# Layer 1's first tile without row gathers behind its exponentials, and the experts' first up weights behind the last 1/sum

## The chip, the cores and the metric

The kernel runs on one core of a Trainium2 chip. The metric is the device time of one execution in microseconds (us). A core has five engines with queues of their own: PE (TensorE, matrix products; its weight loads are listed as PEld), DVE (VectorE), ACT (ScalarE), POOL (GpSimd) and SP (SyncE, which here only issues transfers). Each works through its queue in order; they wait for each other through semaphores.

## The reference, cut to what matters

Four layers. Each adds a cross attention to `x` (4 batches of 512 tokens, 128 wide) and then a mixture of experts; each block reads a layer norm of `x`. The context has 4 batches of 154 rows. The four attentions and expert blocks differ in detail. Layers 1 to 3 look like this:

```python
x = x + xattn(layernorm(x), ctx)     # 16 heads; layer 1: 8 wide, layers 2 and 3: 64 wide
#   energy = q k^T * scale ; attn = softmax(energy) ; out = (attn @ v) @ Wo
x = x + ffn(layernorm(x))            # 8 experts
#   logits = x @ Wg ; the best expert (layer 1) or the best two (layers 0, 2, 3) of each token
#   y = act(x @ W1[e] + b1) @ W2[e] ; out = sum of weight * y
```

Layer 0's experts are gated (two up weights of 128 by 512 and SiLU), those of layers 1 and 3 are 128 by 512 (GELU, ReLU), those of layer 2 128 by 256 (GELU). Everything is float32.

## The kernel before

**Tokens and tiles.** `x` stays in SBUF as four tiles `x[b]` of 128 partitions by 4 by 128. An attention goes through 16 tiles of 128 queries, `(b, i)` with `b` the batch and `i` the quarter of it; they are counted 0 to 15 here.

**The attention of layers 1 to 3.** The class `Tile` holds the steps of one tile. `score(g)` (g = 0, 1, 2) makes the scores of up to six heads on PE; `most(g)` takes minus their row maxima on DVE (L309); `exp(g)` exponentiates them on ACT, head by head, and sums the rows (L323). `inverse` takes 1/sum on DVE (L347). `replicate` brings 1/sum into the shape of the transposed output: a transpose on PE (L352), a copy `rT` on DVE (L354), a transfer `rd` to DRAM and one or two transfers `rep` back that repeat each row for the channels of its head (L359 and L360 in layer 1, L363 and L365 in layers 2 and 3). `turn(n)` transposes four heads' weights on PE (L388), `take(n)` copies them to SBUF as `pT` (L279 on DVE, L282 on ACT), `by_v(n)` multiplies them by the values (L425). `turn_ends`, `take_ends` (`tails`) and `by_v_ends` do that for the last 26 of the 154 context rows. `scaled` multiplies by `rep` (L432, `aT`), `project` is the output projection (L442), `residual` adds to `x`.

**The period.** Two tiles are worked on at a time. `narrow_period` (layer 1) and `wide_period` (layers 2 and 3) write out one period: the scores and exponentials of the new tile between the transposes and products of the old one. In layer 1 a tile's `replicate` comes in the period of the next tile and its projection in the one after that; in layers 2 and 3 `replicate` comes at the end of the tile's own period. `attend_all` loops over the 16 periods. The period calls hooks: `parts` prepares the next batch (norm, keys, values), `middle` and `after` call `step`, which goes one step further in a generator `beside`. In the first periods `beside` is the combination of the layer before, from the tile `(2, 0)` on it is the routing of the first half of the tokens. When `b == 1 and i == 0`, `beside` is finished and the statistics of batches 2 and 3 are taken; the norm of batch 2 stands in `parts` of tile (1, 1).

**The experts.** The tokens are handled in two halves (batches 0 and 1, batches 2 and 3). `route` computes norm, logits, the best experts and each token's slot, and puts one scatter for each tile and choice on the list `rows_due` (L752, an indirect DMA on POOL). `experts` goes through blocks of 128 slots: `load` fetches four blocks of tokens when all scatters are done (L870), `tokens` transposes them on PE (L882), `up` reads the block's expert number into registers of SP and PE, loads this expert's up weights (L901, `w`, three buffers) and multiplies (L909), `down` applies the activation, multiplies by the down weights (L948), copies (L957) and stores to `ybuf` (L960). In layers 1 to 3 two blocks go together (`PER`), a pair; one buffer `w` holds one pair's weights. `load_down` fetches all down weights of a layer in one transfer of 2 MB (1 MB in layer 2; L852).

**Row transfers.** `gather` puts the way back on `rows_due` too: for each tile and choice one indirect DMA on POOL (L993) that fetches the rows from `ybuf`, after all stores. `combine` adds them to `x` with their weights (L1017). `row_transfers(n, behind)` starts the next `n` of the list and makes each of them wait for the instruction `behind`, so that they are spread: two behind each `pT` copy, `2 * n` behind each copy of `down`. In layer 1, three more stand behind each of the three `exp(g)` of tile 0, so that of the 16 gathers of layer 0's second half nine go behind tile 0's exponentials and seven behind the `pT` copies in the period of tile 1.

**Who sets the order.** The program is built with `schedule_with_timeline_sim=True`: a planner orders each engine's queue by its own estimate of times, in favour of what comes first in the program. Within `tc.manual_schedule(engines=...)` the queues named keep the program's order: PE and ACT in the attention of layer 1 (`ordered`), PE, ACT and DVE in that of layers 2 and 3 (`ordered_all`). All else is the planner's: DVE in layer 1's attention, SP and POOL everywhere, and all queues in the experts' stages.

**From the attention to the experts.** After `attend_all` the program starts `experts(layer, 0, ...)` by one step (tokens and the first pair's weights and products), then writes the last tile's remaining period (`narrow_period(None, last, older=late)` or `wide_period(None, last)`; `last` is tile 15 and `late` tile 14), then alternates two steps of the second half's routing with one of the first half's experts.

Of the kernel before, what the change touches and what calls it, by code (L numbers as in the profile page):

```python
# [30 lines left out]
GROUPS = (((0, 1), (2, 3)),) * 4  # L31
# [6 lines left out]
PER = (1, 2, 2, 2)  # L38
# [18 lines left out]
def tile_xattn_moe_stack(ctx: ExitStack, tc: tile.TileContext, a: dict, out: bass.AP):  # L57
# [10 lines left out]
    nc = tc.nc  # L68
# [216 lines left out]
    class Tile:  # L285
# [31 lines left out]
        def exp(self, g):  # L317
            if g == 0:
                self.pr = p2.tile([P, H, S2], F32, tag="probs", name="probs")
            for s in range(min(3, 8 - 3 * g)):  # L320
                for j in range(2):
                    h = self.at.heads(None, 3 * g + s, j)
                    ins = nc.scalar.activation(  # L323
                        self.pr[:, h, :],
                        self.sc[g][:, j, s * S2 : (s + 1) * S2],
                        AF.Exp,
                        bias=self.nm[:, h : h + 1],
                        accum_out=self.rs[:, h : h + 1],
                    )
            if self.at.dh < 64 and self.at.first and self.i == 0:  # L330
                row_transfers(3, ins)

        def short(self):
            if self.nb == 1:
# [14 lines left out]
        def replicate(self):  # L349

            q = ps_tr()
            nc.tensor.transpose(q[0:H, 0:P], self.rinv, ident)  # L352
            rT = small.tile([H, P], F32, tag="rT", name="rT", bufs=2)
            nc.vector.tensor_copy(rT, q[0:H, 0:P])  # L354
            self.rep = p2.tile([P, self.nb, P], F32, tag="rep", name="rep", bufs=1)
            dh = self.at.dh
            if self.nb == 1:
                rd = dram.tile([P, P], F32, tag="rd8", name="rd8", bufs=4)
                nc.sync.dma_start(rd.rearrange("(h d) q -> h d q", d=dh), bc(rT, 1, dh))  # L359
                nc.sync.dma_start(self.rep[:, 0, :], rd)  # L360
            else:
                rd = dram.tile([H, P], F32, tag="rd", name="rd", bufs=4)
                nc.sync.dma_start(rd, rT)  # L363
                for j in range(self.per):
                    nc.sync.dma_start(  # L365
                        self.rep[j * dh : (j + 1) * dh],
                        rd.rearrange("(c j) q -> j c q", j=self.per)[j].partition_broadcast(dh),
                    )


        def turn_ends(self):
# [288 lines left out]
    def row_transfers(n=2 * MOST, behind=None):  # L660

        for start in rows_due[:n]:
            ins = start()
            if behind is not None:
                wait_for(ins, (behind,), "spread over the work beside it")
        del rows_due[:n]
# [185 lines left out]
        nc.sync.dma_start(t[:, :, 0:nf, :], a[f"down{layer}"].rearrange("p (e c d) -> p e c d", e=E, c=nf))  # L852
        return t

    def experts(layer, half, routed, w2):

        ebs, _, scatters = routed
        nj, nf, nu = most_blocks(layer, half), NF[layer], UPS[layer]
        per = PER[layer]
        pack = a[f"up{layer}"]  # L860
# [26 lines left out]
        def up(blocks):  # L887

            w = wff.tile([P, 1032], F32, tag="w", name="w")
            w = w[:, 0 : per * width].rearrange("p (b n) -> p b n", b=per)  # L890
            sc = ps_sc()
            es = []
            for b, j in enumerate(blocks):
                e = nc.values_load(
                    ebs[0:1, j : j + 1],
                    engines=[mybir.EngineType.SP, mybir.EngineType.PE],
                    min_val=0,
                    max_val=E - 1,
                    skip_runtime_bounds_check_because="a count of at most E - 1, by a minimum",
                )  # L900
                nc.sync.dma_start(w[:, b, :], pack[bass.ds(e, 1), :, :].rearrange("o p n -> p (o n)"))  # L901
                es.append(e)
            for b, j in enumerate(blocks):
                xT = toks[j // 4][:, (j % 4) * P : (j % 4 + 1) * P]
                for u in reversed(range(nu)):
                    for fc in range(nf):
                        at = (u * nf + fc) * P
                        dst = sc[:, u if per == 1 else b, fc * P : (fc + 1) * P]
                        nc.tensor.matmul(dst, w[:, b, at : at + P], xT, start=True, stop=True)  # L909
            return es, w, sc  # L910
# [230 lines left out]
    def layer1_setup():  # L1141
# [24 lines left out]

        def prepare(b, found):
            at = Attention()
            at.dh, at.wo, at.first = dh, woT, b == 0

            def masks_in():
                if b == 0:
# [195 lines left out]
    def attend_all(layer, prepare, found, at, beside):  # L1368

        old = older = None
        period = narrow_period if layer == 1 else wide_period
        busy[0] = layer == 1
        with tc.manual_schedule(engines=ordered if layer == 1 else ordered_all):
            new = Tile(at, 0)
            if layer == 1:  # L1380
                new.score(0)
                new.most(0)
            for b in range(B):
                new_at = prepare(b + 1, found) if b < B - 1 else None
                for i in range(NI):
                    at_n, i_n = (at, i + 1) if i < NI - 1 else (new_at, 0)
                    nxt = Tile(at_n, i_n) if at_n else None
                    step = nothing if (b, i) in ((0, 0), (2, 0)) or layer > 1 and (b, i) == (0, 1) else beside.step

                    def queries(i=i, at=at):  # L1390
                        if i < NI - 1:
                            at.queries(i + 1)

                    def parts(i=i, new_at=new_at):
                        if new_at:
                            for part in new_at.parts[i]:
                                part()
                            if i == NI - 1:
                                new_at.queries(0)

                    def after(b=b, i=i, step=step):
                        step()
                        if GROUPS[layer - 1][1][0] == 1 and b == 0 and i == 1:
                            found[1] = stats(x[1])
                        if b == 1 and i == 0:
                            beside.finish()
                            found.update({k: stats(x[k], layer == 2) for k in range(2, B)})

                    period(new, old, nxt, step, queries, parts, after, older)
                    if b == 2 and i == 0:  # L1410
                        beside = Steps(route(layer, 0, *gates[layer]))
                    older, old, new = old, new, nxt
                at = new_at
        busy[0] = False
        return beside.finish(), old, older
# [15 lines left out]
    for layer in range(4):  # L1431
        w2 = load_down(layer)
        if layer == 0:
            result, second = attend_first(layer, prepare, found)
            last = None
        else:
            result, last, late = attend_all(layer, prepare, found, at, beside)
            second = Steps(route(layer, 1, *gates[layer]))
        routed = [result]
        row_transfers()  # L1440
        if 0 < layer < 3:
            prepare = setups[layer + 1]()
        first = Steps(experts(layer, 0, routed[0], w2)).step(2 // PER[layer])
        if layer == 1:
            narrow_period(None, last, older=late)
            last.project()
            last.residual()
        elif last:
            wide_period(None, last)
        while not second.done:  # L1450
            second.step(2)
            first.step(2 // PER[layer])
        routed.append(second.result)
        stores = first.finish()
        row_transfers()
        got = gather(layer, 0, routed[0], stores)
        if layer < 3:
            if layer == 0:
                prepare = setups[1]()
            at = prepare(0, found)  # L1460
            for part in at.early:
                part()
        second = Steps(experts(layer, 1, routed[1], w2)).step((9, 3, 5, 5)[layer])
        for k, b in enumerate(GROUPS[layer][0]):
            for i in range(NI):
                combine(layer, 0, k, i, routed[0], got)
            if layer < 3:
                found[b] = stats(x[b], layer == 1)
            else:
                nc.sync.dma_start(out_v[b], x[b])  # L1470
            second.step(2 // PER[layer])
        if layer < 3:
            for part in at.late:
                part()
            at.queries(0)
        stores = second.finish()
        beside = Steps(combining(layer, routed[1], gather(layer, 1, routed[1], stores)))
# [33 lines left out]
```

## Time and profile before

| what | value |
|---|---|
| median of 6 runs | 1266.0 us (1263.77 to 1272.77) |
| the profiled execution | 1272.21 us, its span 1270.5 us |
| mean granted TensorE clock | 0.932 |
| busy share of the span | PE 85%, PEld 70%, DVE 57%, ACT 44%, POOL 20% |
| chain that ended last | PE 59%, DVE 14%, DMA 9%, issue 7%, POOL 5%, ACT 5% |
| layer 1's attention, first and last scores (L1236) | 253.7 to 465.5 us |
| the 16 gathers in it (L993) | first issued at 264.7, last at 284.6 us |
| first expert products (L909) of layers 1, 2, 3 | 470.58, 798.55, 1133.35 us |

A row of a timeline gives start, duration, engine, line, operation and output<-inputs, how many instructions were merged, and in brackets how long the engine had been idle before it and what ended that. A row of the chain of waits gives start, duration and who. Instructions of DMA on SP and POOL are the issues; the landing comes later. Times are from the span's start.

### The profile page before, as it was taken

Reading aid. Unit: us, or ns where it says so; the run is one execution under the profiler, and the core shown is the slowest. Engines: PE = TensorE matmul, PEld = TensorE weight load, DVE = VectorE, ACT = ScalarE, POOL = GpSimd, SP = SyncE. Lnnn points to the kernel's source line nnn. Section 1 sums busy time; section 2 is a strip of 40 time slices with the busy share of each in tenths; the row PEclk is TensorE's granted clock in tenths of the full one; section 3 lists DMA queues with packets and bytes.
Section 4 is the critical chain, followed back from the end, with each engine's and each line's share of the span. In section 5 each row is a group of like instructions: output and inputs, shape, how many; then the busy total and the mean of one; then the engine's idle time right before and its main releaser. Section 6 shows DMA issues by size and latency. Waiting matters only on the chain.

```text
span 1270.5 us, 26420 instructions
## 1 busy us (share of the span) xinstructions
PE 1085.5 (85%) x9412; PEld 890.8 (70%) x9412; DVE 730.1 (57%) x2012; ACT 564.2 (44%) x2264; POOL 252.6 (20%) x281
## 2 busy tenths in 40 slices
PE   6877998958878788879999998976899999899990
PEld 4657997924444457778878777865778787789880
DVE  6655547567776753235666776524476576646352
ACT  2204333454554554346556565321656665532220
POOL 2041405050000200212000013045220000402334
PEclk9788999988998988989999999887899999999996
DMA  7025776630011313532112214444421111444762
GB/s 230 1 78 151 223 237 187 207 114 12 13 25 34 86 50 110 158 110 52 35 36 67 51 39 122 136 148 128 126 56 43 43 35 36 110 108 139 214 182 60
DMA packets 136064, 126.77 MB, mean 100 GB/s; under 512 B 12538, under 2 KB 115583, under 8 KB 135551
## 3 DMA queue, kind: packets, MB, share of 16 engines
q1 hardware_dynamic: 128767, 110.39, 31.0%
q0 software_dynamic: 7168, 14.69, 4.0%
q8 instruction: 77, 1.26, 0.4%
q14 instruction: 52, 0.43, 0.1%
HBM read 101.31 MB, written 23.72 MB: 98 GB/s over the span
## 4 chain that ended last, share of the span: by engine, by line
PE 59%; DVE 14%; DMA 9%; issue 7%; POOL 5%; ACT 5%; SPq 2%; POOLq 0%; DVEq 0%; ACTq 0%
PE sc L909 10%; PE av L948 7%; PE tr L388 6%; PE av L425 6%; PE sc L625 5%; PE tr L442 5%; DMA yg<-ybuf,su 3%; PE sc L610 3%; ACT probs L323 3%; DVE nm L309 3%; POOL yg L993 3%; PE sc L1236 2%; DMA w<-in_up 2%; POOL buf L752 2%; PE av L407 2%
## 5 line engine op out<-in xcount | busy, mean ns | idle before, releaser
L323 ACT ACTIVATE probs<-sc,nm 128x154 f32<-128x154 f32 x768 | 286.3, 402 | 163.3 <-DVE nm L309 161.4
L909 PE MATMUL sc<-tokT,w 128*128 128x128 f32 x1528 | 198.8, 283 | 12.9 <-DMA w<-in_up 6.5
L909 PEld LDWEIGHTS sc<-tokT,w 128*128 128x128 f32 x1528 | 186.9, 198 | 18.7 <-ACT eg L932 5.9
L309 DVE TENSOR_REDUCE nm<-sc 128x6 f32<-128x924 f32 x144 | 142.6, 1007 | 70.6 <-PE sc L625 47.6
L323 ACT ACTIVATION_READ_ACCUMULATOR probs<-sc,nm 128x1 f32 x768 | 168.4, 219 | 0.0
L948 PE MATMUL av<-w,hT 128*128 x1160 | 155.9, 279 | 3.3 <-DVE hT L937 2.7
L993 POOL DMA_INDIRECT yg<-ybuf,su x112 | 107.0, 956 | 244.5 <-issue 68.5
L948 PEld LDWEIGHTS av<-w,hT 128*128 128x128 f32 x1160 | 141.7, 192 | 9.1 <-issue 4.0
L752 POOL DMA_INDIRECT buf<-xn,su x112 | 108.3, 967 | 199.1 <-DVE ve L248 55.3
L250 POOL TENSOR_TENSOR rstd<-ve,nhalf 128x4 f32<-128x4 f32 x32 | 32.9, 1029 | 567.8 <-DVE ve L248 510.0
L279 DVE COPY pT<-tr 128x512 f32<-128x512 f32 x160 | 106.8, 684 | 43.9 <-PE tr L388 40.1
L388 PE MATMUL tr<-ident,probs 128*128 128x128 f32 x768 | 121.8, 289 | 7.8 <-DVE rT L354 7.8
L425 PE MATMUL av<-pT,vm 128*64 128x128 f32 (+1 forms) x1536 | 106.3, 284 | 19.4 <-DVE pT L279 19.3
L388 PEld LDWEIGHTS tr<-ident,probs 128*128 128x128 f32 x768 | 85.1, 145 | 39.4 <-issue 21.3
L425 PEld LDWEIGHTS av<-pT,vm 128*64 128x64 f32 (+1 forms) x1536 | 63.8, 127 | 52.6 <-DVE pT L279 27.4
L932 ACT ACTIVATE eg<-sc,w 128x128 f32<-128x128 f32 x184 | 52.9, 367 | 88.3 <-PE sc L909 83.7
L625 PE MATMUL sc<-kT,qT 64*128 64x154 f32 x1024 | 86.2, 305 | 4.7 <-ACT probs L323 4.7
L625 PEld LDWEIGHTS sc<-kT,qT 64*128 64x128 f32 x1024 | 70.5, 187 | 15.7 <-issue 9.9
L937 DVE SCALAR_TENSOR_TENSOR hT<-sc,w,eg 128x128 f32<-128x128 f32 x184 | 55.9, 341 | 41.1 <-ACT eg L932 41.1
L610 PE MATMUL sc<-xnT,wq 128*128 128x128 f32 x512 | 72.8, 301 | 4.7 <-ACT probs L323 2.3
L610 PEld LDWEIGHTS sc<-xnT,wq 128*128 128x128 f32 x512 | 66.5, 210 | 10.0 <-issue 3.4
L957 DVE COPY ys<-av 128x256 f32<-128x256 f32 (+1 forms) x110 | 38.9, 355 | 54.5 <-PE av L948 50.6
(260 smaller groups left out, 1462.6 us busy)
## 6 DMA issues: line engine op xcount, KB each, us to landing
w<-in_up SPq DMA_DIRECT2D x46, 516.0 KB
w<-in_up SPq DMA_DIRECT2D x76, 258.0 KB
rep<-rd SPq DMA_DIRECT2D x64, 256.0 KB
tok<-buf SPq DMA_DIRECT2D x36, 256.0 KB
ybuf<-ys SPq DMA_DIRECT2D x58, 128.0 KB
w<-in_down SPq DMA_DIRECT2D x3, 2048.0 KB
w<-in_up SPq DMA_DIRECT2D x46, 128.0 KB
ybuf<-ys SPq DMA_DIRECT2D x52, 64.0 KB
```

The lines of the kernel that those rows point to most:

```text
L279: return nc.vector.tensor_copy(o, i)
L309: nc.vector.tensor_reduce(self.at.heads(self.nm, g, n), self.sc[g][:, :, 0 : n * S2].rearrange("p j (s k) -> p j s k", s=n), AX.X, ALU.max ...
L323: ins = nc.scalar.activation(self.pr[:, h, :], self.sc[g][:, j, s * S2 : (s + 1) * S2], AF.Exp, bias=self.nm[:, h : h + 1], accum_out=self ...
L388: nc.tensor.transpose(q[:, t * P : (t + 1) * P], self.pr[:, h, 0:P], ident)
L425: nc.tensor.matmul(av[rows, cols], v, self.pT[n][:, t, :], start=False, stop=last)
L442: nc.tensor.matmul(o[:, 0:D], self.aT[:, c, :], self.at.wo[:, c, :], start=(c == 0), stop=(c == self.nb - 1))
L610: nc.tensor.matmul(sc[:, c // 4, c % 4 * P : (c % 4 + 1) * P], wq[:, c * P : (c + 1) * P], at.xnT[:, i * P : (i + 1) * P], start=True, sto ...
L625: nc.tensor.matmul(sc[:, j, s * S2 : (s + 1) * S2], at.qT[i][rows, c, :], at.kT[rows, c, :], start=True, stop=True)
L752: ins = nc.gpsimd.indirect_dma_start(out=buf[half], out_offset=bass.IndirectOffsetOnAxis(ap=su[:, t : t + 1], axis=0), in_=xns[t // NI][:, ...
L909: nc.tensor.matmul(dst, w[:, b, at : at + P], xT, start=True, stop=True)
L948: nc.tensor.matmul(y[:, b * D : (b + 1) * D], hT[:, fc, :], w2[:, bass.ds(es[b], 1), fc, :].rearrange("p o d -> p (o d)"), start=(fc == 0) ...
L993: ins = nc.gpsimd.indirect_dma_start(out=yg[:, i % NI, :], out_offset=None, in_=ybuf[half][0 : most_blocks(layer, half) * P, :], in_offset ...
```

## The change

Four edits, in the language of the kernel:

1. `Tile.exp` no longer starts row transfers behind the exponentials of layer 1's first tile. The gathers of layer 0's second half now all go two at a time behind `pT` copies: eight in the period of tile 1, eight in that of tile 2.
2. In `attend_all`, `step` does nothing in tile (0, 1) of layer 1 either, as it already did in layers 2 and 3. Layer 0's combination advances in the periods of tiles 2 and 3 instead of 1 and 2.
3. `replicate` keeps its `rep` transfers in `self.sent`. `experts` has a new argument `ahead`; the up loads of the first three pairs of the first half wait for those transfers: tile 14's in layer 1, tile 15's in layers 2 and 3. In layer 0 there are none.
4. A line in `after` goes whose condition (`GROUPS[layer - 1][1][0] == 1`) holds in no layer, since `GROUPS` is ((0, 1), (2, 3)) for all of them.

```diff
@@ Tile.exp
-                    ins = nc.scalar.activation(
+                    nc.scalar.activation(
...
-            if self.at.dh < 64 and self.at.first and self.i == 0:
-                row_transfers(3, ins)
@@ Tile.replicate
-                nc.sync.dma_start(self.rep[:, 0, :], rd)
+                self.sent = [nc.sync.dma_start(self.rep[:, 0, :], rd)]
             else:
...
-                for j in range(self.per):
+                self.sent = [
                     nc.sync.dma_start(
                         self.rep[j * dh : (j + 1) * dh],
                         rd.rearrange("(c j) q -> j c q", j=self.per)[j].partition_broadcast(dh),
                     )
+                    for j in range(self.per)
+                ]
@@ experts
-    def experts(layer, half, routed, w2):
+    def experts(layer, half, routed, w2, ahead=()):
...
-                nc.sync.dma_start(w[:, b, :], pack[bass.ds(e, 1), :, :].rearrange("o p n -> p (o n)"))
+                ins = nc.sync.dma_start(w[:, b, :], pack[bass.ds(e, 1), :, :].rearrange("o p n -> p (o n)"))
+                if j < 3 * per:
+                    wait_for(ins, ahead, "the transfers of the attention's last tile go first")
@@ layer1_setup, prepare
-            at.dh, at.wo, at.first = dh, woT, b == 0
+            at.dh, at.wo = dh, woT
@@ attend_all
-                    step = nothing if (b, i) in ((0, 0), (2, 0)) or layer > 1 and (b, i) == (0, 1) else beside.step
+                    step = nothing if (b, i) in ((0, 0), (0, 1), (2, 0)) else beside.step
...
-                        if GROUPS[layer - 1][1][0] == 1 and b == 0 and i == 1:
-                            found[1] = stats(x[1])
@@ the loop over layers
-        first = Steps(experts(layer, 0, routed[0], w2)).step(2 // PER[layer])
+        ahead = (late if layer == 1 else last).sent if last else ()
+        first = Steps(experts(layer, 0, routed[0], w2, ahead)).step(2 // PER[layer])
```

## The prediction

> **What bounds the kernel now.** Part 4 of the page (the chain that ended last) puts 59% of the span on PE, 14% on DVE and 9% on transfers, but that is an average over four layers; the change touches four places, so I read those. First the table of busy time by stretch, for the start of layer 1's attention; its columns after the width are PE, PEld, DVE, ACT, POOL, the granted clock, DMA share and GB/s.
>
> ```profile
> 262.00:289.00 27.00, 15.76 (x94) 7.25 (x92) 18.55 (x54) 9.86 (x48) 17.07 (x18) 0.76 0.18 50
> 289.00:302.00 13.00, 11.26 (x85) 6.36 (x85) 8.74 (x21) 6.79 (x33) 0.26 (x1) 0.83 0.06 11
> 339.00:351.00 12.00, 9.62 (x85) 4.93 (x85) 8.56 (x17) 6.80 (x33) 0.00 (x0) 1.00 0.06 11
> ```
>
> A later period of this attention takes 11 to 14 us; the one from 262 to 289 takes 27, with no engine full. So something waits there. The chain of waits and the timelines of DVE and PE say what:
>
> ```profile
> 256.27 7.34 DMA ybuf<-ys
> 264.71 0.71 POOL yg L993
> 267.28 0.35 DVE L1017 SCALAR_TENSOR_TENSOR x<-yg,wa,x 128x128 f32<-128x128 f32 x1 [3.83 <-DMA yg<-ybuf,su]
> 270.02 1.11 DVE L309 TENSOR_REDUCE nm<-sc 128x6 f32<-128x924 f32 x1
> 271.05 0.27 DVE L354 COPY rT<-tr 16x128 f32<-16x128 f32 x1
> 271.38 1.11 PE L388 MATMUL tr<-ident,probs 128*128 128x128 f32 x4 [6.96 <-DVE rT L354]
> 284.30 0.65 PE L425 MATMUL av<-pT,vm 128*32 128x128 f32 x8 [3.90 <-DVE pT L279]
> ```
>
> Layer 0's last expert store lands 7.3 us after its issue, behind the 2 MB load of down weights (L852, issued 0.4 us earlier). The row gathers then start one by one, 1.25 us apart. Layer 0's combination (L1017) stands in DVE's queue ahead of the second tile's maxima (L309) and of rT (L354), whose input PE had finished at 263.98. DVE stands still for the rows, and PE stands 6.96 us behind DVE, then 3.90 us more.
>
> Second, the moment where attention hands over to the experts, in layer 2 (queue of SP, PE, POOL):
>
> ```profile
> 771.58 1.19 SPq L901 DMA_DIRECT2D w<-in_up  x2
> 793.03 1.26 SPq L365 DMA_DIRECT2D rep<-rd  x2
> 799.74 6.38 SPq L901 DMA_DIRECT2D w<-in_up  x8
> 798.55 1.16 PE L909 MATMUL sc<-tokT,w 128*128 128x128 f32 x8
> 808.16 1.16 PE L442 MATMUL tr<-wo,aT 128*128 128x128 f32 x8
> 826.43 1.02 POOL L752 DMA_INDIRECT buf<-xn,su  x1 [14.27 <-DVE eb L775]
> 850.75 1.97 PE L882 MATMUL tr<-ident,tok 128*128 128x128 f32 x8 [6.32 <-DMA tok<-buf]
> ```
>
> The first three pairs of up weights (six loads) are in SBUF 20 us before use. PE has expert products (L909) between the last tile's turns, and that tile's last projection (L442) ends only at 809.3. Behind it run the second half's routing, its 16 scatters (20 us on POOL) and its tokens; PE waits 6.32 us for those. Layers 1 and 3 have the same shape, with shorter waits:
>
> ```profile
> 470.58 2.02 PE L909 MATMUL sc<-tokT,w 128*128 128x128 f32 x16 [0.40 <-issue]
> 526.37 0.66 PE L882 MATMUL tr<-ident,tok 128*128 128x128 f32 x4 [2.59 <-DMA tok<-buf]
> 1133.35 2.05 PE L909 MATMUL sc<-tokT,w 128*128 128x128 f32 x16
> 1190.11 0.66 PE L882 MATMUL tr<-ident,tok 128*128 128x128 f32 x4 [1.96 <-DMA tok<-buf]
> ```
>
> **Part 1: gathers and combination.** Nothing is removed but order: 16 gathers, 16 L1017 and the statistics behind them are all still done. Nine gathers lose their place behind tile 0's exponentials (tiles counted from 0, so the table's 27 us are mostly the period of tile 1); in return all 16 go two by two behind the pT copies (L279) of the periods of tiles 1 and 2, and the combination's steps move from tile 1's period to those of tiles 2 and 3.
>
> What goes. (a) The stand before rT: from 263.98 to 271.05, 7.0 us. In the new order rows cannot be asked for before tile 0's first pT copy, so no L1017 can stand before rT or tile 1's second maxima. (b) The rest of tile 1's period: rT to rT is 18.16 us (271.05 to 289.21); the next two are 13.63 and 13.19. I take 13.2 for it: 5.0 us. Together 12.0.
>
> What comes back. 16 L1017 at 0.35 us (5.6) and 8 pairs of L241 and L243 at 0.29 and 0.18 (3.8) are 9.4 us of DVE work. DVE's free time is 4.3 us in the stretch 289 to 302, 4.0 in 302 to 316, and about 13.2 - 8.6 = 4.6 in a normal tile 1: 12.9 in all. It fits, but DVE is in order and each of these can stand before a copy that PE waits for. Bounds: nothing, or all 9.4 us. I take 2.0, about six of the L1017 in the way, nearer to nothing because the room is there. Gain of part 1: 12.0 - 2.0 = 10.0, between 2.6 and 13 (12, and up to 1 where PE ran at half clock: the records grant 0.5 from 269.5 to 276.3 and 283.1 to 293.3).
>
> What hides it: the store's late landing is covered, since it landed at 264.0 and tile 0's first pT copy ends about 266.0 (263.98 plus 0.27, 0.67 and 0.68 for rT, tails and pT, and their handovers). POOL: behind the gathers stand only two rstd (L250), wanted a period later. The gathers will end near 288 instead of 285.5; the combined batches 2 and 3 are first needed by the norm in tile 5's period, after 327. If the rows came later than the order supposes, DVE would stand again: that is the slower rival below.
>
> **Part 2: the held weights.** Six loads each in layers 1, 2 and 3 now wait on SP for a rep transfer to land. Behind a waiting SP stand token groups 2 and 3 (796.38 and 798.06 in layer 2, read at 816.1), later stores, and in layer 1 tile 15's rd and rep (L359, L360; 473.7, 476.1). Those could be up to 2.2 us late (six loads at 0.85 us from 467.7 end at 472.8); rep landed at 478.2 and is read at 486.1, so nothing.
>
> The cost if nothing covers it, from landings in the trace's semaphore records and SP's 0.85 us for each load (four at 425.0 take 2.83 with the last one's 0.33). Layer 1: rep landed 467.7, second load of pair 0 issued 468.6, landed 2.7 later at 471.3, against 470.58: 0.7. Layer 2: rep's second half issued 793.66, landing after 4.3 to 5.4, so near 799; second load at 800, landed 2.1 later at 802.1, against 798.55: 3.5. Layer 3: rep landed 1134.5, second load 1135.4, landed 2.8 later at 1138.2, against 1133.35: 4.9. In all 9.1 us of late experts.
>
> The cover is the attention's last tile, which PE has to do anyway. In layer 2 5.6 us of L909 and L948 lie between 798.55 and L442's end; in layer 3 9.7 us. If these go behind, the last residual and with it the second half's routing, scatters and tokens come earlier, by the 3.5 to 4 us of layer 2 (wait there 6.32), by no more than the 2.5 us of waits for tokens in layer 3 (1.96 and 0.56), and by no more than 2.6 in layer 1: up to 9.1. So part 2 lies between -9.1 and +9.1. I take +1 for layer 1, +2 for layer 2, 0 for layer 3 (PE is 25.92 us busy of the 26 from 1130, so what is moved must be paid there): +3, on the side where a wait is known to be there to be shortened.
>
> [...]
>
> **Sum.** 10 + 3 = 13 us. The profiled execution took 1272.2 (span 1270.5, 1.7 around it), so 1259 for it; it is 6.2 over the median of the six runs, 1266.0, so 1253 for the median. 0.3% is 3.8 us, about what a measurement of this kernel can tell.
>
> **The rivals.** A, the hold is exposed: PE's queue keeps L909 ahead of the last tile's steps, the in-order PE stands for the weights, 9.1 us, and attention stands behind it. Gain 10 - 9.1, time about 1265, between 1260 and 1268. For it: in layer 3 no idle time exists to pay with. Against: the queue order is planned anew, and the planner knows of the wait.
>
> B, slower: the wait for rows is moved, not removed. DVE's queue is in order; if the build places each L1017 right behind the pT copy that releases its rows, DVE stands the gather's 0.3 + 2.5 us (2.4 to 2.5 from issue to landing) at each of 8 pairs: 22 us against 12 saved, 10 slower with part 2 at nothing, 1276. It decides from 5 of the 8 pairs on (14 us). For it: L1017 stands for rows nine times today, 7.8 us. Against: today's order did not know of the late store, which no longer counts.
>
> C, the stand is partly the profiled run's own: that execution is 6.2 over the median. If unprofiled runs have half of the 7.0 and 5.0, the change removes half of what it says: part 1 gives 6 - 2 = 4, with part 2 7, the time is 1259.
>
> **How the numbers follow.** Forecast 0.70 (1246 to 1260 by itself), A 0.13, B 0.09, C 0.08. Forecast and C are faster, A is so at one end (0.05 of its 0.13): faster 0.83; A's other 0.08 same; B 0.09 slower. The range 1246 to 1266 takes in the forecast, C and over half of A, and leaves out B and the tails.
>
> **What would show it.** Right: no L1017 between 262 and 266; rT of tile 0 near 264.3 and then periods of 12 to 14 us; PE's 6.96 and 3.90 gone; in layer 2 six w loads behind rep, L442's end 3 us closer to rT, and the wait of 6.32 shorter. Wrong: a period over 16 us among tiles 1 to 3 (B), PE idle at its first L909 for w in layers 2 and 3 with L442 as late as now (A), or L1017 waits that total over 14 us.

## The result: slower, and the profile after

The changed kernel takes 1277.0 us (median), the kernel before beside it 1268.3: the ratio is 1.0069, with a 95% interval of 1.0053 to 1.0084. The forecast was 13 us faster. The profiled execution after spans 1275.5 us, the one before 1270.5. These are 5.0 us apart and the medians 8.7, since the profiled execution of before (1272.21) lies 3.9 above its median of 1268.3; what follows accounts for the 5.0.

Tables of times in both traces, measured from the same steps, show where they lie. "First scores" is PE's first L1236 (after: L1238), rT the DVE copy L354 (after: L352). Below the diff lines after stand two higher than before: L909 is L911, L948 is L950, L1017 is L1019; above them some stand two lower.

| stretch | before | after | difference |
|---|---|---|---|
| start to first scores of layer 1 | 253.68 | 251.81 | -1.87 |
| first scores to rT of tile 3 | 62.35 | 59.37 | -2.98 |
| to rT of layer 2's first tile | 263.12 | 263.51 | +0.39 |
| layer 2's attention | 212.15 | 212.13 | -0.02 |
| last rT of layer 2 to first of layer 3 (experts; below, layer 2's step) | 118.34 | 121.39 | +3.05 |
| layer 3's attention | 218.00 | 218.16 | +0.16 |
| last rT of layer 3 to the end of the last addition (experts; below, layer 3's last stage) | 139.11 | 145.48 | +6.37 |

The first row lies before anything that the change acts on; in the profiles of e5 to e8 (below) it is 249.9 to 253.6. So the new place of the gathers gave 3.0 us in this profile, and the expert stages of layers 2 and 3 took 9.4 back.

**Layer 1's first tiles.** The table of busy time by stretch for the periods of tiles 1 to 3 and, for comparison, of tile 6 (width, then PE, PEld, DVE, ACT, POOL, granted clock, DMA share, GB/s):

```profile
262.98:278.66 15.68, 10.83 (x81) 4.92 (x81) 10.86 (x29) 7.73 (x40) 7.62 (x8) 0.89 0.17 42
278.66:295.45 16.79, 11.51 (x85) 5.40 (x85) 13.23 (x41) 6.71 (x33) 8.82 (x9) 0.79 0.15 40
295.45:311.18 15.73, 13.42 (x85) 6.77 (x85) 10.79 (x24) 7.26 (x35) 1.03 (x1) 0.79 0.05 9
334.51:346.34 11.83, 9.62 (x85) 4.93 (x85) 8.39 (x17) 6.72 (x33) 0.00 (x0) 1.00 0.06 11
```

The one long period of before (18.16) is gone, and the two behind it, 13.63 and 13.19 before, have become 16.8 and 15.7. The timelines of POOL, DVE and PE show a different picture from before's: rT comes at once, and the waits are now inside the periods.

```profile
264.97 0.99 POOL L995 DMA_INDIRECT yg<-ybuf,su  x1 [44.64 <-DVE pT L279]
262.98 0.27 DVE L352 COPY rT<-tr 16x128 f32<-16x128 f32 x1
267.63 0.35 DVE L1019 SCALAR_TENSOR_TENSOR x<-yg,wa,x 128x128 f32<-128x128 f32 x1 [1.19 <-DMA yg<-ybuf,su]
276.97 0.35 DVE L1019 SCALAR_TENSOR_TENSOR x<-yg,wa,x 128x128 f32<-128x128 f32 x1 [0.97 <-DMA yg<-ybuf,su]
274.25 0.43 PE L425 MATMUL av<-pT,vm 128*32 128x128 f32 x8 [2.80 <-DVE pT L279]
289.26 0.66 PE L425 MATMUL av<-pT,vm 128*32 128x128 f32 x8 [2.83 <-DVE pT L279]
```

The view of waits for 255 to 312 us sums them (total, times, longest). DVE still stands for rows ten times; PE stands behind DVE, now for pT instead of rT:

```profile
DVE x L1019 <- DMA yg<-ybuf,su: 7.2, 10, 1.2
PE av L425 <- DVE pT L279: 7.8, 4, 2.8
```

**Layers 2 and 3.** In the timelines of SP and PE, the w loads now stand behind rep, and PE stands for them (the first two rows are SP's queue in layer 2, then PE in layer 2 and in layer 3):

```profile
788.48 1.26 SPq L363 DMA_DIRECT2D rep<-rd  x2
794.02 1.27 SPq L901 DMA_DIRECT2D w<-in_up  x2
796.14 0.68 PE L911 MATMUL sc<-tokT,w 128*128 128x128 f32 x4 [1.92 <-DMA w<-in_up]
807.75 1.16 PE L442 MATMUL tr<-wo,aT 128*128 128x128 f32 x8
849.68 2.22 PE L882 MATMUL tr<-ident,tok 128*128 128x128 f32 x8 [6.21 <-DMA tok<-buf]
1132.07 0.66 PE L388 MATMUL tr<-ident,probs 128*128 128x128 f32 x4
1135.98 3.79 PE L911 MATMUL sc<-tokT,w 128*128 128x128 f32 x16 [3.26 <-DMA w<-in_up]
1150.00 1.06 PE L442 MATMUL tr<-wo,aT 128*128 128x128 f32 x8
```

The last projection of layer 3 before, for comparison:

```profile
1146.65 1.06 PE L442 MATMUL tr<-wo,aT 128*128 128x128 f32 x8
```

In layer 2 PE's order around L911 is that of before; in layer 3 one group of the last tile's turns (the L388 at 1132.07) went ahead of L911, and no more. The last projection (L442) starts 20.9 us behind the last rT in layer 2 (rT at 786.82; before 16.9) and 23.6 in layer 3 (rT at 1126.36; before 19.0): 4.1 and 4.6 us later, where the forecast had it 3 earlier in layer 2. In layer 1 PE's first products wait for no weights (L911 at 465.76, 0.39 idle for `issue`, as 0.40 before). The wait for tokens stayed at 6.21. And the 16 products of 1135.98 took 3.79 us, where before they took 2.05: the granted clock is 0.5 from 1134.8 to 1141.7, from 1.2 us before the wait of 3.26 ends. In layer 2 it is 0.5 from 796.9 to 800.3, from 0.8 us behind the end of the wait of 1.92. Before has neither stretch at these places. (Over all of layer 2's step, though, both traces have the same time at 0.5, 37.5 and 37.4 us: before has 6.8 us of it at 815.6, after 3.4 at 817.4.)

### The profile page after: what moved, and what is told of

It is laid out like the page before. It is cut to its first block, busy times and chain, and to the rows that moved or that the text cites. A ratio compares the mean times of both kernels' runs of the same rounds, so it can differ in the third digit from the quotient of the medians.

```text
span 1275.5 us, 26418 instructions
## 1 busy us (share of the span) xinstructions
PE 1090.5 (85%) x9412; PEld 893.0 (70%) x9412; DVE 730.2 (57%) x2012; ACT 564.6 (44%) x2264; POOL 252.5 (20%) x281
## 5 line engine op out<-in xcount | busy, mean ns | idle before, releaser
L323 ACT ACTIVATE probs<-sc,nm 128x154 f32<-128x154 f32 x768 | 286.3, 402 | 156.1 <-DVE nm L309 155.9
L911 PE MATMUL sc<-tokT,w 128*128 128x128 f32 x1528 | 203.1, 287 | 17.9 <-DMA w<-in_up 9.4
L911 PEld LDWEIGHTS sc<-tokT,w 128*128 128x128 f32 x1528 | 190.9, 202 | 23.7 <-DVE tokT L103 6.3
L950 PE MATMUL av<-w,hT 128*128 x1160 | 155.1, 278 | 3.1 <-DVE hT L939 2.1
L950 PEld LDWEIGHTS av<-w,hT 128*128 128x128 f32 x1160 | 141.3, 192 | 8.8 <-issue 4.3
L388 PE MATMUL tr<-ident,probs 128*128 128x128 f32 x768 | 122.4, 289 | 1.5 <-DVE rT L352 1.5
L388 PEld LDWEIGHTS tr<-ident,probs 128*128 128x128 f32 x768 | 85.2, 145 | 33.5 <-issue 22.0
L425 PEld LDWEIGHTS av<-pT,vm 128*64 128x64 f32 (+1 forms) x1536 | 63.9, 127 | 54.2 <-DVE pT L279 29.1
L625 PEld LDWEIGHTS sc<-kT,qT 64*128 64x128 f32 x1024 | 70.8, 188 | 15.7 <-issue 9.9
```

Of the source, the lines that this page charges most:

```text
L323: nc.scalar.activation(self.pr[:, h, :], self.sc[g][:, j, s * S2 : (s + 1) * S2], AF.Exp, bias=self.nm[:, h : h + 1], accum_out=self.rs[:, ...
L388: nc.tensor.transpose(q[:, t * P : (t + 1) * P], self.pr[:, h, 0:P], ident)
L425: nc.tensor.matmul(av[rows, cols], v, self.pT[n][:, t, :], start=False, stop=last)
L625: nc.tensor.matmul(sc[:, j, s * S2 : (s + 1) * S2], at.qT[i][rows, c, :], at.kT[rows, c, :], start=True, stop=True)
L950: nc.tensor.matmul(y[:, b * D : (b + 1) * D], hT[:, fc, :], w2[:, bass.ds(es[b], 1), fc, :].rearrange("p o d -> p (o d)"), start=(fc == 0) ...
```

## Experiments

The kernels e1 to e4 and e9 to e11 ran on chips where the kernel before takes 1345 and 1338 us, e5 to e8 on one where it takes 1270; times are compared only with the kernel before on the same chip.

**The two halves apart.** The first kernel has the gathers alone, the second the hold alone.

```diff
 e1 (after, but)
-        ahead = (late if layer == 1 else last).sent if last else ()
+        ahead = ()
 e2 (after, but)
+            if self.at.dh < 64 and self.at.first and self.i == 0:
+                row_transfers(3, ins)
...
-                    step = nothing if (b, i) in ((0, 0), (0, 1), (2, 0)) else beside.step
+                    step = nothing if (b, i) in ((0, 0), (2, 0)) or layer > 1 and (b, i) == (0, 1) else beside.step
...
```

> The change without the hold (ahead is always empty); PE, ACT and SP keep their order of before, only DVE and POOL in layer 1's first tiles differ. Theory H (the loss is the held weights' wait on PE, the gathers gain a little): rT of tile 3 some 3 us earlier after layer 1's first scores than before, as in the changed kernel, everything later as before; 3 us faster than before, 0.997 to 0.999. Rival G (the gathers' new place is the loss, and the profile of before was a slow one there): no earlier or later at tile 3, 3 to 8 us slower than before, 1.003 to 1.006.

> The hold alone; gathers and combination as before. Theory H: PE waits for w at its first L909 in layers 2 and 3 by 2 and 3 us and then runs at half clock for some us; from tile 31 to tile 32 3 us longer, from tile 47 to the end 6 us longer, 9 to 12 us slower than before, 1.007 to 1.010. Rival G: the hold is covered, within 3 us of before.

Measured: the gathers alone 0.9947 (0.9925 to 0.9969), the hold alone 1.0081 (1.0058 to 1.0104). Theory H holds, and the gathers were worth a little more than it said. PE's rows where layer 3 hands over (first products, last projection), the gathers alone first, with the last rT at 1188.73, then the hold alone, with it at 1190.05:

```profile
1195.69 2.05 PE L911 MATMUL sc<-tokT,w 128*128 128x128 f32 x16
1208.99 1.06 PE L442 MATMUL tr<-wo,aT 128*128 128x128 f32 x8
```

```profile
1199.88 3.83 PE L913 MATMUL sc<-tokT,w 128*128 128x128 f32 x16 [1.82 <-DMA w<-in_up]
1213.11 1.06 PE L444 MATMUL tr<-wo,aT 128*128 128x128 f32 x8
```

Layer 3's last stage is 149.9 us without and 159.2 with the hold. The two ratios multiply to 1.0028 where the whole change has 1.0069; the runs are on different chips, and what the difference is isn't shown.

**Where the hold costs.** The gathers, and the hold in layer 3 alone.

```diff
-        ahead = (late if layer == 1 else last).sent if last else ()
+        ahead = (late if layer == 1 else last).sent if last and layer == 3 else ()
```

> The gathers' new place in layer 1 as in the change, and the six held loads in layer 3 alone; layers 1 and 2 issue their first up weights early, as before. The gathers alone ran at 0.9947 of before. Theory H3 (the hold costs where PE reaches the first up products before the weights do, and there mostly in layer 3, whose wait of 3.26 us is followed by 6.8 us at a granted clock of 0.5): 6 to 9 us come back, the ratio to before is 1.000 to 1.002, and the wait for w of 2 to 3 us stands in PE's rows of layer 3 alone. Rival E (the three layers pay about alike): a third of the 1.3% between the two halves of the change, 0.998 to 0.9995.

Measured: 1.0023 (1.0001 to 1.0045). Between 0.9947 for the gathers alone and 1.0069 for the whole change lie 1.2%; the hold in layer 3 alone accounts for about 0.8 of it, more than half of it from one layer, and the interval lies above rival E's range. That is H3, though the ratio is just above its 1.000 to 1.002. Its PE has the same wait in layer 3, and the records grant 0.5 from 1129.1 for 6.8 us:

```profile
1130.17 4.03 PE L911 MATMUL sc<-tokT,w 128*128 128x128 f32 x16 [3.40 <-DMA w<-in_up]
```

Layer 2's step is back at 118.5 us (after 121.4), layer 3's last stage is 144.6 (before 139.1).

**The order of PE's queue.** The wait for w costs because PE's order, fixed when the kernel is built, has the first products ahead of the last tile's steps. This edit moves the experts' first step behind the last tile's period in layers 2 and 3; it was made without the hold (e4, and e9 on another chip) and with it (e6).

```diff
-        first = Steps(experts(layer, 0, routed[0], w2, ahead)).step(2 // PER[layer])
+        first = Steps(experts(layer, 0, routed[0], w2, ahead))
+        if layer < 2:
+            first.step(2 // PER[layer])
...
         elif last:
             wide_period(None, last)
+            first.step(2 // PER[layer])
```

> The change without the hold, and in layers 2 and 3 the experts' first step is written after the last tile's remaining period, so that PE's order has the last tile's turns and products before the experts' products. Theory O (an earlier end of the last tile brings the second half's routing, scatters and tokens forward): last projection 3 to 4 us earlier in layer 2 and PE's wait for the second half's tokens shorter by as much; 2 to 4 us faster than the kernel without the hold in layer 2, 0 to 2 in layer 3. Rival P (PE's own work is the bound, and the order only moves it): the last projection is earlier but the second half's first product is not, within 2 us in each layer.

> The whole change, with one edit more: in layers 2 and 3 PE's order takes the attention's last tile first and the first expert products behind it. Theory Q (the hold costs only because PE's queue keeps the first expert products ahead of the last tile's steps, so that PE stands): the weights are in SBUF before PE asks, no wait for w over 0.5 us is left in layers 2 and 3, and the ratio to before is 0.992 to 0.996, as it was for the same order without a hold (0.9928). Rival L (the late transfers cost by themselves, since every later weight load of the stage moves back with them): the hold's 10 us stay whatever the order, 0.999 to 1.003.

Measured without the hold: 0.9928 (0.9906 to 0.9949), an interval that overlaps that of the gathers alone. In the profile the last projection of layer 3 starts 10.0 us behind rT instead of 20.3, and the stage behind it is 144.9 us instead of 149.9; layer 2's step is 134.4 instead of 132.9. In that pair of profiles the order did more than Theory O had for layer 3, and nothing of what it had for layer 2.

Measured with the hold: 0.9942 (0.9919 to 0.9966). This is what settles the cause: the whole change, loads held just as late, goes from 1.0069 to 0.9942 by PE's order alone. Theory Q holds, L falls. PE's rows of the kernel with the hold, in layer 3 (last rT at 1121.76), and SP's queue:

```profile
1129.53 1.16 PE L442 MATMUL tr<-wo,aT 128*128 128x128 f32 x8 [0.53 <-DVE aT L432]
1132.06 1.16 PE L442 MATMUL tr<-wo,aT 128*128 128x128 f32 x8 [0.20 <-DVE aT L432]
1133.06 1.95 PE L911 MATMUL sc<-tokT,w 128*128 128x128 f32 x16
1123.75 1.26 SPq L363 DMA_DIRECT2D rep<-rd  x2
1128.79 4.54 SPq L901 DMA_DIRECT2D w<-in_up  x6
```

Both last projections are done 11.5 us behind rT, the first 16 products take 1.95 us (2.05 in before) without a wait, and no clock of 0.5 is granted from 1115 to 1200. (Its later waits for w, 1.08 and 0.61 us, are at the second half's pairs, which are not held; before has two of 0.94 and 0.85 such.) The stretch of 17 us from the last rT in layer 3 says it in one line each, for before, after and this kernel:

```profile
1127.63:1144.63 17.00, 16.92 (x160) 15.00 (x159) 7.23 (x19) 4.04 (x11) 0.00 (x0) 1.00 0.52 126
```

```profile
1126.36:1143.36 17.00, 13.66 (x103) 12.09 (x102) 4.79 (x13) 2.90 (x7) 0.00 (x0) 0.80 0.58 159
```

```profile
1121.76:1138.76 17.00, 16.19 (x156) 14.38 (x155) 9.48 (x27) 3.19 (x9) 1.04 (x1) 1.00 0.60 160
```

PE's matmul records are 160, 103 and 156: after loses a third of PE's work in this stretch, to 3.3 us of standing and 6.8 at the clock of 0.5. With the order, layer 2's step is 114.9 us and layer 3's last stage 133.6, so 3.4 and 5.5 less than before. For layer 3 this is the order's gain and not the held loads': e4 and e8, with the order and no hold, have 5.0 less than e1 and 5.2 less than before. For layer 2 it isn't shown: no kernel on this chip has the order there without the hold, on the other chip e4's step was 1.5 us longer than e1's, and e6 has 30.7 us at 0.5 in that step instead of 37.5, which alone could be the 3.4 (half of the 6.8 between them, an estimate).

> The gathers' place as in the change, no hold, and PE's order with the attention's last tile first in layer 3 alone. With it in layers 2 and 3 the ratio was 0.9928, and in that profile layer 3 from the last rT to the end was 5 us shorter than with the gathers alone, the step from layer 2's last rT to layer 3's first 1.5 us longer. Theory T (the order pays in layer 3 only): 0.990 to 0.993. Rival U (it pays in layer 2 and 3 alike, the 1.5 us were other transfers): 0.993 to 0.996.

Here the order was changed in layer 3 only, without a hold: 0.9943 (0.9921 to 0.9964). In the profile layer 3's last stage is 133.9 us and layer 2's step 118.5, as before. The time falls in rival U's range, but the interval reaches into both, and what the order alone adds to the gathers (0.9947 on another chip) is too small to be told from the times; that it shortens layer 3's stage by 5.2 us is a reading of single profiles.

> The gathers' place as in the change, no hold, attention's last tile first in PE's order in layers 2 and 3: the kernel that ran at 0.9928 on another chip, here beside the next two. The whole change with that order ran at 0.9942, its layer 2 from last rT to layer 3's first rT 3.4 us shorter than before's. Theory N (with that order the hold neither costs nor gains): 0.992 to 0.996, layer 2's step 114 to 116 us as with the hold. Rival M (the hold itself gives layer 2 its 3.4 us, by letting rep and tokens through first): layer 2's step stays at 118 us or more, and it is 2 to 4 us slower than the next kernel's order would give, 0.995 to 0.998.

Measured: 0.9929 (0.99 to 0.9957), within Theory N. Its step of layer 2 took 129.3 us, and 131.5 in the kernel with the hold on this slower chip (e11, below), so the numbers of 114 to 118 didn't apply; e10 below, without a hold and otherwise like e11, has 130.6. The hold does not shorten the step, which speaks against M. No kernel with the old order was profiled on this chip, so its stages (layer 3's last one is 151.8 to 156.1 us in e9 to e11) can't be compared with before's.

**Where part 1's gain went.** Two kernels with the gathers alone. In the first, DVE's steps stand in program order in layer 1's first batch, so that the combination comes late (`order.to(e)` opens `manual_schedule` for the engines `e`).

```diff
-        with tc.manual_schedule(engines=ordered if layer == 1 else ordered_all):
...
+        order.to(ordered_all)
...
+            if b == 1 and layer == 1:
+                order.to(ordered)
```

> The change without the hold, and in layer 1's first batch DVE keeps the program's order too, so that each group of eight L1017 stands at the end of the period after its gathers. Theory W (what part 1 loses is DVE waiting for rows, because the planner places L1017 too early): no wait of L1017 for yg in the periods of tiles 1 to 3, rT 0 to rT 3 in 40 to 44 us instead of 48.2 in the changed kernel, 8 to 11 us faster than before, 0.991 to 0.994. Rival D (DVE's own work of 9.4 us is what lengthens these periods, wherever it stands): rT 0 to rT 3 stays at 47 to 49 us, as in the kernel without the hold.

Measured: 1.0015 (0.9993 to 1.0036); from rT of tile 0 to that of tile 3 it is 48.9 us (50.2 in e1). Theory W falls: no L1019 waits, and the periods are as long. DVE's timeline shows one reason: the additions with their statistics, in a row, are in front of the next maxima and of rT.

```profile
297.64 0.34 DVE L1019 SCALAR_TENSOR_TENSOR x<-yg,wa,x 128x128 f32<-128x128 f32 x1
300.39 0.34 DVE L1019 SCALAR_TENSOR_TENSOR x<-yg,wb,x 128x128 f32<-128x128 f32 x1
300.65 1.12 DVE L309 TENSOR_REDUCE nm<-sc 128x6 f32<-128x924 f32 x1
302.33 0.27 DVE L352 COPY rT<-tr 16x128 f32<-16x128 f32 x1
```

The median is above e1's, while the profile ends within 0.4 us of e1's, with first scores 4.8 us earlier. The profiles differ most behind these tiles: from rT of tile 9 to rT of tile 13 it is 69.0 us in e3 and 61.1 in e1. Why isn't shown.

> The gathers alone, with the 16 additions of layer 0's expert rows (scalar_tensor_tensor in combine) left out, so layer 0's second half of the expert output isn't added; gathers and statistics stay. Theory D (the combination on DVE's in-order queue, 5.6 us of additions and their 7 us of waits for rows, is what makes the periods of tiles 1 to 3 15.7, 16.8 and 15.7 instead of 13.2): from rT of tile 0 to rT of tile 3 it takes 40 to 43 us, and the ratio is 0.988 to 0.992. Rival S (these periods are long because of the next batch's setup beside them and the clock at 0.5 in two or three stretches): 46 to 49 us, 0.993 to 0.996.

```diff
+        if (layer, half) == (0, 1):
+            return
         for (cw, _), yg in zip(routed[1], got[k].rows):
             nc.vector.scalar_tensor_tensor(xi, yg[:, i, :], cw[:, t : t + 1], xi, ALU.mult, ALU.add)
```

Measured: 0.9919 (0.9888 to 0.995). Theory D holds and was still too cautious: from rT of tile 0 to that of tile 3 36.8 us, 11.5 less than after. The same table for its tiles 1 to 3:

```profile
264.70:275.83 11.13, 9.17 (x81) 4.51 (x81) 7.98 (x16) 7.75 (x40) 7.00 (x8) 1.00 0.19 47
275.83:288.24 12.41, 9.62 (x85) 4.93 (x85) 9.07 (x21) 6.73 (x33) 8.19 (x9) 1.00 0.22 59
288.24:301.45 13.21, 10.37 (x85) 5.14 (x85) 9.20 (x19) 7.27 (x35) 0.00 (x0) 1.00 0.07 16
```

POOL's eight gathers stand in each of the first two periods as in after, and the periods are short beside them. What cost is the 16 additions on DVE, and the clock beside them: after has 17 us at 0.5 between 262 and 312 (274.7 to 278.1, 288.3 to 302.0), and without the additions the clock stays at 1.00. The waits for rows alone are not it, since e3 had none and its periods were as long; how the 11.5 us divide between DVE's time and the clock isn't shown.

**A version that takes the additions off DVE.** POOL can do them in two steps each; e10 does so on top of e9, e11 on top of e6.

```diff
+            if (layer, half) == (0, 1):
+                nc.gpsimd.tensor_scalar(yg[:, i, :], yg[:, i, :], cw[:, t : t + 1], None, ALU.mult)
+                nc.gpsimd.tensor_tensor(xi, yg[:, i, :], xi, ALU.add)
+                continue
             nc.vector.scalar_tensor_tensor(xi, yg[:, i, :], cw[:, t : t + 1], xi, ALU.mult, ALU.add)
```

> The kernel before it in this list, with layer 0's 16 additions in layer 1's first tiles done by POOL as a tensor_scalar and a tensor_tensor each, behind its gathers, instead of by DVE. Without the additions the three periods were 36.8 us and no clock of 0.5 was granted beside them. Theory D2 (it is DVE's in-order queue that the additions and their rows hold up): rT of tile 0 to rT of tile 3 in 36 to 41 us, no clock of 0.5 there, 7 to 11 us faster than without, 0.984 to 0.989. Rival K (POOL's steps take longer than DVE's 0.35 us, and the rows come late for the norm and the routing behind them, or slow DVE's own copies): the periods stay at 46 us or more, or a period behind tile 4 grows by as much, 0.993 to 1.003.

> The whole change with attention's last tile first in layers 2 and 3, and layer 0's 16 additions on POOL. Theory N and D2 together: as the kernel before it, 0.984 to 0.989, with the first three periods at 36 to 41 us and no wait for w over 1.2 us in layers 2 and 3. Rival M: 2 to 4 us faster than the kernel before it. Rival L (the hold costs beside any order): 5 us or more slower than it.

Measured: 0.9942 (0.9924 to 0.9961) without the hold, 0.9916 (0.9888 to 0.9944) with it; beside them e9, without POOL's part, 0.9929. None of the three can be told from the others, so D2 falls on the time, and K is nearer. In e11 the three periods are 45.4 us together, and its longest wait for w is 0.97. The table says why, for the three periods of the kernel without the hold:

```profile
269.85:282.68 12.83, 9.71 (x81) 4.72 (x81) 7.97 (x15) 7.73 (x40) 9.23 (x13) 0.94 0.18 42
282.68:296.40 13.72, 11.80 (x85) 6.53 (x85) 9.15 (x22) 6.72 (x33) 11.95 (x17) 0.81 0.18 44
296.40:315.38 18.98, 12.26 (x85) 5.62 (x85) 14.65 (x36) 7.25 (x35) 12.94 (x22) 0.82 0.08 18
```

Tiles 1 and 2 have their short periods (16.0 and 16.8 in e9), and tile 3 pays it back (15.4 in e9): POOL runs late, its rstd holds up DVE's norm by 1.31 us, and the norm's four steps take 3.72 us beside POOL's additions (1.11 in after, at 297.39, with POOL idle):

```profile
305.22 3.72 DVE L257 TENSOR_SCALAR xn<-x,mv,rstd 128x128 f32<-128x128 f32 x4 [1.31 <-POOL rstd L250]
306.36 2.49 POOL L1021 TENSOR_TENSOR x<-yg,x 128x128 f32<-128x128 f32 x6
```

By their ratios all kernels with the attention's last tile first beat both the kernel before and the changed one, by under 1% against before; the whole change in that order, with POOL's additions or without, is at 0.992 to 0.994.

## Why the prediction was wrong

**Part 2 failed at one choice.** The prediction worked out the price of the uncovered hold as 0.7, 3.5 and 4.9 us, 9.1 in all, and took +3 instead, "on the side where a wait is known to be there to be shortened". The profile has 3.0 and 6.4 in layers 2 and 3, 9.4 in all, and no wait for weights in layer 1: rival A's mechanism, place and price. The argument against A, that the order is planned anew and the planner knows of the wait, was not evidence from the profile, and it failed: the new order still had L911 of the first pair ahead of all of the last tile's steps that it had been ahead of, but for one group of four turns in layer 3. Nor did PE's busy time cover the wait in layer 2, 16.86 us of the 17 from 795 to 812 before:

```profile
795.00:812.00 17.00, 16.86 (x157) 14.76 (x155) 7.36 (x17) 5.39 (x8) 0.87 (x1) 1.00 0.53 142
```

From L909 at 798.55 on, that work stood in PE's queue at and behind the instruction that now waits. Experiment e6 shows what that meant, since with the last tile in front the same held loads cost nothing.

Within the price the terms were sized wrongly in both directions. L911 starts 2.1 us later behind rT in layer 2 and 3.9 in layer 3 (9.32 against 7.25, 9.62 against 5.72), less than 3.5 and 4.9. The sum had no term for the clock of 0.5 that came with the wait: 6.8 us of it in layer 3, where 16 products took 3.79 us instead of 2.05, are by an estimate from these up to 3.4 us of lost work, enough for the other 2.5 of its 6.4. In layer 2, 0.9 of the 3.0 stay unaccounted for, since over its whole step the time at 0.5 did not grow.

**Part 1 had its mechanism right and a term wrong.** (a), the stand before rT, is gone: 6.2 us between the first scores and rT of tile 0, of 7.0. (b) is half there: tile 1's period is 15.7, not 13.2. "What comes back" was taken as 2.0, "nearer to nothing because the room is there"; of 12.0 us 3.0 were left in the profile, so 9.0 came back, near the bound of 9.4: 3.3 of (a) and (b) never left, and the periods of tiles 2 and 3 grew by 3.2 and 2.5. Room in the sum of DVE's free time is not room in an in-order queue whose every copy has PE behind it. Rival B was half there: a period over 16 us came (16.8), and waits for rows of 7.2 us, below the 14 that B asked for. e7 shows that it hangs on the additions on DVE, with the clock beside them.

**What stays open.** The gathers alone are 0.3 to 0.75% faster, 3.9 to 9.5 us of 1266; the first tiles show 3.0 in one pair of profiles and 2.1 in the other (e2 against e1, first scores to rT of tile 3: 66.0 and 63.9). The second is smaller by up to 2.5 because in e1 the clock is at 0.5 in tile 0's scores: its rT comes 13.7 us behind the first scores, in e4 and e8 too, and 11.2 in after and the others with this place of the gathers but e3. Where the rest is from isn't shown. Rival C (the stand partly the profiled run's own) is not borne out: e2, which has the old place of the gathers, has rT of tile 0 17.2 us behind the first scores, before has 17.4.

**The starting point.** The kernel before measures 1268.3 here, not 1266.0, which is 2 us of the 24 between the forecast and the result.

## What to carry to other kernels

A transfer that is held back costs what the in-order engine that needs it has queued behind the instruction that waits; look up that order in the built program before you count busy time as cover, and when a load is held, move its first reader behind other work in the same edit. Moving waits and short steps about on an in-order engine can pay back most of what it saves, here 9 of 12 us, if another engine waits for nearly every step on it, even where its busy time leaves room. Price a new wait on PE with the clock that may come with it (here 3.4 us at 0.5 with a wait of 1.92, 6.8 with one of 3.26), not with its own length alone.

## What the runs showed of the hardware

Four waits of PE for w came with a granted clock of 0.5. Those of 1.92 and 1.82 us (layer 2 after, layer 3 in e2) came with one stretch of 3.4 us, those of 3.26 and 3.40 us (after, e5) with one of 6.8. Between the last rT of layer 3 and 1190, before, e6 and e8, whose first products had no wait, have none.

The same pause doesn't always bring it. In all 13 kernels PE pauses for 1.13 and 1.31 us at the same two places in layer 1's first scores. In five of them (e1 to e4 and e8) a stretch at 0.5 begins 6.5 to 7.8 us behind the first score, in the other eight none does before 15 us; the same four products take 1.91 us in e8 and 1.04 in after:

```profile
260.31 1.91 PE L1238 MATMUL sc<-kz,qT 64*128 64x462 f32 x4
259.37 1.04 PE L1238 MATMUL sc<-kz,qT 64*128 64x462 f32 x4
```

All 13 wait 2.3 us for rinv just ahead of the last rT in layer 3; at that place e1 to e3 and e9 to e11 show 3.4 us at 0.5, the other seven none.

DVE's steps took longer beside POOL's additions: in e10 the four xn steps (L257) at 305.22, beside six additions on POOL (2.49 us from 306.36 on), took 3.72 us together, and the four of after at 297.39, with POOL idle, 1.11. No run here separates POOL's work from other causes.
